# The last image's depthwise convolution with its tiles in turn, its layernorm in two parts, weight factors on ScalarE and one product block moved later

## The chip, the core and the metric

The kernel runs on one core of a Trainium2 chip. Its time is device time in microseconds (us) for one execution. Before the change it is 3458.06 us, the median of three runs (3454.50 to 3460.47). All numbers of a profile come from one more execution, which the profiler recorded.

Engines are called by their short names: PE (TensorE, matrix products), DVE (VectorE), ACT (ScalarE), POOL (GpSimd) and SP (SyncE, which issues almost all DMAs). Each engine takes its own instructions in program order.

## What is computed

Two layers follow each other on 8 images of 384 channels and 32 x 32 pixels, all in float32. Layer 0 is a transformer block over the 1024 pixels of an image. Layer 1 is a ConvNeXt block with a 7 x 7 depthwise convolution and a global response normalization (GRN). Cut to what matters here:

```python
# layer 0, for each image: tokens n = 1024, channels c = 384, 8 heads of 48
x1 = x + proj(softmax(q @ k.T * scale) @ v)        # q, k, v from layernorm(x)
x  = x1 + gelu(layernorm(x1) @ w_fc1 + b_fc1) @ w_fc2 + b_fc2   # hidden 1536
# layer 1, for each image
y = depthwise_conv7x7(x, dw_w) + dw_b              # 49 taps for each channel
y = layernorm(y) * ln_w + ln_b                     # over channels
y = gelu(y @ w1 + b1)                              # hidden 1536
gx = sqrt(sum(y * y, over pixels)); nx = gx / (mean(gx) + eps)
y = gamma * (y * nx) + beta + y
out = x + y @ w2 + b2
```

The GRN makes the last product wait for the whole image: `nx` needs the sum of squares over all pixels. The kernel does not multiply `y` by `1 + gamma * nx`, but the rows of w2, which is the same.

## The kernel before

Channels lie on partitions: an image is three tiles (`CT` = 3) of 128 channels by 1024 pixels. PE multiplies 128 x 128 weights with at most 512 pixels at a time; one such float32 product is counted as `U` = 0.857 us in the code and appears as two MATMUL records in the trace. Layer 1 of an image (here called block b) is worked on while layer 0 of the next image runs, so that DVE's convolution lies beside PE's attention. For the last image (block 7) nothing follows beside which its convolution could lie. That end of the program, from 3000 us on, is what the change is about.

**What sets the order.** Every engine's order is fixed when the program is built, by the class `Flow`. It counts PE time (`flow.pe(us)` after each matmul). Other work is written as generators ("chains") that yield how many us of PE time are to pass before their next step; a chain's next instructions are emitted when PE's count has come that far. `flow.finish(chain)` emits what is left of a chain at once. So a yield time that is too short for the engine makes it fall behind PE, and one that is too long leaves it idle. A chain started by `after(first, chain)` begins when `first` is through.

**The convolution** (L777 to L789) is 49 taps for each of three tiles. Each tap is one DVE instruction on the zero-padded image `pad`: dst = window * tap + dst (L788; the first, L786, adds the bias). For blocks 0 to 6 it runs over whole tiles of 1024 pixels in the order tap by tap, and in each tap over the three tiles (`acc` in the trace). Block 6's taps are spaced 1.5 us of PE time apart (`start_conv`), the first 10 taps of each tile 1.35 times as much.

For block 7 the destination is `last` (a view of the tile `wqkv`, whose weights are no longer needed). The last image's layer 0 MLP runs by halves of the pixels (`mlp_by_halves`, L746): first fc1 and fc2 for pixels 0 to 511, then for 512 to 1023. After each of its three output tiles, DVE evicts PE's bank into `x` (L708), ACT copies the half tile into `pad` (L704), and `between(h, ct)`, which is `last_convolution` (L1217), starts a chain with all 49 taps of that tile for the rows that have become possible: rows 0 to 12 in the first half (416 pixels), rows 13 to 31 in the second (608). Each chain waits for the one before, so the 49 taps of one tile follow one another, each on the result of the one before. After the last fc1 product of the first half, `between(0, -1)` calls `next_norms(7)`, which finishes block 6's convolution and starts its layernorm.

**The layernorm** (L331): two DVE adds over the three tiles (L344, L345), a matmul with ones for the sum over partitions (ln_sum, L348), three DVE subtractions (L352), three ACT squares (L357), two DVE adds (L361, L362), a matmul (ln_var, L365), ACT's Ln and Exp (L373, L374, which need a table load of ACT), three DVE products (L377). `abreast` runs two of them step by step together, the second in borrowed space. The last image's pixels are cut in three parts, `LAST`, of 416, 288 and 320 pixels. The first part has its own layernorm (norm_a), the other two go abreast when the convolution is over (norm_b).

**The end of the program on PE:** block 6's up-projection (h, L296; `grn_up_straight`), block 7's up-projection of the first 416 pixels (h_last, L936; `last_up`), block 6's down-projection (o, L892; `grn_down_straight`: three row blocks r by two halves, each 12 products, with the rows in pairs of weight tiles A11 A12, A21 A22, A31 A32), block 7's up-projection of the 288 and 320 pixels alternating (36 products of each), then block 7's down-projection in nine blocks. After each up-projection matmul group ACT does a Gelu (L328) and a square with a running sum (L869, L942), which gives GRN's sums. `grn_scale` (L945) then takes the square root on ACT, sums over partitions on PE (gxsum, L951), makes the factor on DVE (gmean to gscale, L954 to L959), and `scaled` (L966) multiplies each w2 tile by it on DVE (L969, 128 x 768).

**Memory that gates the order:** weights pass through a ring of 9 tiles; `weights.used` frees one and SP issues the load of the next in the plan. PSUM has four banks for half tiles (`o_tile`) and two double banks (`linear`), handed out in turn, so a matmul group waits until the group four (or two) before it has been read. The residual rows pass through three `res` tiles.

The lines that call these at the end:

```python
                norm_b = flow.spawn(after(state["conv"], last_norm(*LAST[1:])))
                y, gx = grn_up_straight(b - 1, acc, weights, b - 1)
                scale = flow.spawn(grn_scale(b - 1, gx, weights, b - 1, RAW[:2]))
                flow.finish(state["norm_a"])
                ...
                last_up(last, y_last, LAST[:1], sums, weights, f"{b}_0")
                flow.finish(scale)
                ...
                grn_down_straight(b - 1, halves, kept.pop(b - 1), weights, b - 1, b - 1)
        flow.finish(state["conv"])
        flow.finish(norm_b)
        last_up(last, y_last, LAST[1:], sums, weights, f"{B - 1}_1")
        ...
        flow.finish(grn_scale(B - 1, gx, weights, B - 1, RAW[:2]))
        grn_down_straight(B - 1, y_last, kept.pop(B - 1), weights, B - 1, B - 1, LAST)
```

Of the kernel before, what the change touches and what calls it, by code (L numbers as in the profile page):

```python
# [47 lines left out]
ALU = mybir.AluOpType  # L48
# [82 lines left out]
def block_kernel(  # L131
# [75 lines left out]
    def image(ap):  # L207
        return ap.rearrange("p (h w) -> p h w", h=H)
# [537 lines left out]
    def mlp_by_halves(b, xt, xn, weights, ln, rest, between):  # L746

        hid = one.tile([P, HT * N], F32, tag="big", name=f"hid_{b}").rearrange("p (m n) -> p m n", m=HT)
        for h in range(2):
            wa, wb = f"fc1_{b}_{h}", f"fc2_{b}_{h}"  # L750
            flow.finish(ln)
            for m in range(HT):
                gelu_half(hid, m, h, xn, weights, wa, f"fc1_{b}")
                if m % CM == CM - 1:
                    weights.used(wa, m // CM)
                if m == 3 and h == 0:
                    rest()
                    ln = flow.spawn(layernorm(xt, xn, 1, eps0, "g2", f"ln2_{b}", True))
            if h == 0:
                between(0, -1)  # L760
            for ct in range(CT):
                keys = RAW[2 * ct : 2 * ct + 2]
                tiles = [weights.at(wb, key)[:, k, :] for key in keys for k in range(6)]
                ps = linear_half(lambda k: tiles[k], lambda k: hid[:, k, :], HT, h, f"fc2_{b}_{ct}_{h}")
                for key in keys:
                    weights.used(wb, key)
                add_first(xt, ct, h, ps)
                pad_half(xt, ct, h)
                between(h, ct)
# [4 lines left out]
        nc.sync.dma_start(out=kept.rearrange("(c p) n -> p c n", p=P), in_=xt)  # L774
        return kept

    def convolution(acc, us, slow=0, y0=0, y1=H, tiles=range(CT)):  # L777

        for i in range(KS * KS):
            dy, dx = divmod(i, KS)  # L780
            for ct in tiles:
                window = pad[:, ct, dy + y0 : dy + y1, dx : dx + W]
                dst = image(acc[:, ct, :])[:, y0:y1, :]
                tap = col("dww", ct * KS * KS + i)
                if i == 0:
                    nc.vector.tensor_scalar(dst, window, tap, col("dwb", ct), ALU.mult, ALU.add)  # L786
                else:
                    nc.vector.scalar_tensor_tensor(dst, window, tap, dst, ALU.mult, ALU.add)  # L788
                yield us * (1.35 if i < slow else 1.0)  # L789

    def block_differences(acc):

# [77 lines left out]
            weights.used(f"w1_{tag}", i, "A")  # L870
        return y, gx

    def grn_down_straight(b, y, kept, weights, tag, index, parts=(slice(0, NH), slice(NH, N))):

        todo = [(r, part) for r in range(CT) for part in parts]
        res = {}

        def load():
            if len(res) < len(todo):
                r, part = todo[len(res)]  # L880
                t = three.tile([P, NH], F32, tag="res", name=f"res_{b}_{r}_{part.start}")[:, : part.stop - part.start]
                nc.sync.dma_start(out=t, in_=kept[r * P : (r + 1) * P, part])
                res[len(res)] = t

        for _ in range(3):
            load()
        for n, (r, part) in enumerate(todo):
            keys = RAW[2 * r : 2 * r + 2]
            tiles = [weights.at(f"w2_{tag}", key)[:, k, :] for key in keys for k in range(HT // 2)]
            ps = o_tile(f"o2_{b}_{r}")[:, : part.stop - part.start]  # L890
            for k in range(HT):
                nc.tensor.matmul(out=ps, lhsT=tiles[k], rhs=y(k, part), start=(k == 0), stop=(k == HT - 1))  # L892
                flow.pe(U * (part.stop - part.start) / NH)
                if k == 2 and part is parts[0] and r + 1 < CT:
                    for key in RAW[2 * r + 2 : 2 * r + 4]:
                        scaled(b, weights.at(f"w2_{tag}", key), key)
            if part is parts[-1]:
                for key in keys:
                    weights.used(f"w2_{tag}", key)
            nc.vector.scalar_tensor_tensor(res[n], ps, b2[:, r : r + 1], res[n], ALU.add, ALU.add)  # L900
            nc.sync.dma_start(out=image_of(out, index)[r * P : (r + 1) * P, part], in_=res[n])
            load()
# [22 lines left out]

        return at

    def last_up(acc, y, parts, gx, weights, tag):

        for i in range(HT // 2):  # L930
            raw = weights.at(f"w1_{tag}", i, "A")
            for m, tiles in ((i, (0, 1, 2)), (i + HT // 2, (5, 3, 4))):
                for part in parts:
                    ps = o_tile(f"h_last_{m}_{part.start}")[:, : part.stop - part.start]
                    for k in range(CT):
                        nc.tensor.matmul(  # L936
                            out=ps, lhsT=raw[:, tiles[k], :], rhs=acc[:, k, part], start=(k == 0), stop=(k == CT - 1)
                        )
                        flow.pe(U * (part.stop - part.start) / NH)
                    other_table(y(m, part), ps, AF.Gelu, bias=b1[:, m : m + 1])  # L940
                    sums = gx[:, LAST.index(part), m : m + 1]
                    nc.scalar.activation(ps, y(m, part), AF.Square, accum_out=sums)  # L942
            weights.used(f"w1_{tag}", i, "A")

    def grn_scale(b, gx, weights, tag, first=("A31", "A32")):  # L945

        wb = f"w2_{tag}"
        other_table(gx, gx, AF.Sqrt)
# [10 lines left out]
        nc.vector.tensor_scalar(scale, scale, 1.0, None, ALU.add)  # L959
        row_scale[b] = scale  # L960
        for key in first:
            scaled(b, weights.at(wb, key), key)

    row_scale = {}

    def scaled(b, w, key):  # L966
        s = (int(key[2]) - 1) * HT // 2
        factors = row_scale[b][:, s : s + HT // 2].unsqueeze(2).to_broadcast((P, HT // 2, P))
        nc.vector.tensor_tensor(w, w, factors, ALU.mult)  # L969
        return w  # L970
# [169 lines left out]
    def main():  # L1140
# [18 lines left out]
        for b in range(1, B):  # L1159
# [6 lines left out]
            if b == B - 1:  # L1166
                plan += plan_w1(f"{b}_0", False)
            plan += plan_w2(b - 1, b < B - 1)
        weights = Weights(plan + plan_w1(f"{B - 1}_1", False) + plan_w2(B - 1, False))

        t = three.tile([P, 2, NH], F32, tag="p", name="wqk_beta1").rearrange("p a n -> p (a n)")[:, : 2 * C]
        for k in range(CT):
# [12 lines left out]
            state["acc"] = one.tile([P, CT, N], F32, tag="acc", name=f"acc_{b}")  # L1185
            state["conv"] = flow.spawn(convolution(state["acc"], us, slow), paced=True)

        def next_norms(b):

            if b > 0:  # L1190
                acc = state["acc"]
                flow.finish(state["conv"])
                norm = abreast(acc, acc, eps1, "lnw", f"ln3_{b - 1}", True)
                state["norm3"] = flow.spawn(sequence(norm, block_differences(acc)) if b < B - 1 else norm)
            if b + 1 < B:
                xn = state["xn"] = load_x(b + 1, "xn")
                state["norm1"] = flow.spawn(
# [10 lines left out]

        last = wqkv[:, : CT * N].rearrange("p (c n) -> p c n", c=CT)

        def last_norm(*parts):
            args = last, last, eps1, "lnw", f"ln3_{B - 1}", True
            if len(parts) == 2:
                return abreast(*args, parts=parts)
            return layernorm(*args[:2], *parts, *args[2:], slow=2.0)

        def last_convolution(h, ct):  # L1217
            if ct < 0:
                next_norms(B - 1)
                return  # L1220
            rows = (LAST[0].stop // W, H) if h else (0, LAST[0].stop // W)
            state["conv"] = flow.spawn(
                after(state["conv"], convolution(last, 0.86 if h else 0.6, 0, *rows, (ct,))), paced=True
            )
            if (h, ct) == (0, CT - 1):
                state["norm_a"] = flow.spawn(after(state["conv"], last_norm(LAST[0])))

        for b in range(B):
            qT, kT, last_tile = qk(b, state["xn"])
# [19 lines left out]
            flow.finish(state["norm3"])  # L1249
            if b < B - 1:  # L1250
                y, y1, gx = grn_up(b - 1, acc, weights, b - 1)
                start_conv(b, 1.5 if b == B - 2 else 1.8, 10)
                scale = flow.spawn(grn_scale(b - 1, gx, weights, b - 1))
                next_values(b + 1)
                flow.finish(scale)
                grn_down(b - 1, y, y1, kept.pop(b - 1), weights, b - 1, b - 1)
            else:

                norm_b = flow.spawn(after(state["conv"], last_norm(*LAST[1:])))
                y, gx = grn_up_straight(b - 1, acc, weights, b - 1)  # L1260
                scale = flow.spawn(grn_scale(b - 1, gx, weights, b - 1, RAW[:2]))
                flow.finish(state["norm_a"])
                sums = small.tile([P, CT, HT], F32, tag="gx_last", bufs=1, name="gx_last")
                y_last = places()
                last_up(last, y_last, LAST[:1], sums, weights, f"{b}_0")
                flow.finish(scale)
                halves = lambda k, part: y[:, k, part]
                grn_down_straight(b - 1, halves, kept.pop(b - 1), weights, b - 1, b - 1)
        flow.finish(state["conv"])
        flow.finish(norm_b)  # L1270
        last_up(last, y_last, LAST[1:], sums, weights, f"{B - 1}_1")
        gx = sums[:, 0, :]
        for i in range(1, CT):
            nc.vector.tensor_tensor(gx, gx, sums[:, i, :], ALU.add)
        flow.finish(grn_scale(B - 1, gx, weights, B - 1, RAW[:2]))
        grn_down_straight(B - 1, y_last, kept.pop(B - 1), weights, B - 1, B - 1, LAST)

    engines = {nc.tensor.engine, nc.vector.engine, nc.scalar.engine, nc.gpsimd.engine, nc.sync.engine}
    with tc.manual_schedule(engines=engines):
# [129 lines left out]
```

## Time and profile before

| what | value |
|---|---|
| median of the runs | 3458.06 us |
| profiled execution: its time, its span | 3456.23 us, 3454.4 us |
| mean granted PE clock | 0.994 of full speed |
| PE busy in the span | 3390.3 us (98%) |
| DVE busy | 2510.1 us (73%) |
| ACT busy | 1293.2 us (37%) |
| DVE busy from 3171.7 to 3322.5 us | 145.3 of 150.8 us |
| PE busy in the same stretch | 132.3 us, clock 0.94 |
| first matmul of block 7's down-projection, end of its last | 3382.58 us, 3446.46 us |

The span is the time from the first to the last instruction of the profiled execution; its time is 1.8 us more. A line of a timeline gives the start in us from the span's start, the duration of the group, engine and line of the code, the operation, and what is written and read (tile names, partitions x elements), with the number of instructions; in square brackets stands how long the engine was idle before, and whose end released it. In a list of waits the columns are who waited, for whom, the sum in us, how often, and the longest. A row by stretches has the stretch, its length, the busy time of an engine with the number of instructions, and the granted PE clock, 1.00 being full speed.

### The profile page before, as it was taken

What the parts mean: (1) busy time and instruction counts of PE and PEld (TensorE: products, weight loads), DVE (VectorE), ACT (ScalarE), POOL (GpSimd) and SP (SyncE); (2) the same over time, 40 slices, a digit from 0 to 9 for tenths busy, and PEclk for the clock granted to TensorE, in tenths of its full rate; (3) what the DMA queues carried; (4) which work ended last, traced back from release to release, by engine and by line L of the source; (5) the groups of instructions that cost most, each with busy time, mean ns of one, the idle gap of its engine ahead of it and who ended that gap; (6) DMA issues with size and microseconds to landing.
All of it is one profiled execution on the core that took longest, in us unless ns stands there. A gap on an engine that the chain in (4) does not pass through costs nothing.

```text
span 3454.4 us, 36387 instructions
## 1 busy us (share of the span) xinstructions
PE 3390.3 (98%) x14278; PEld 1454.9 (42%) x14278; DVE 2510.1 (73%) x3100; ACT 1293.2 (37%) x1669; POOL 23.0 (1%) x45
## 2 busy tenths in 40 slices
PE   8999999999999999999999999999999999999988
PEld 3444434443344433444334443444434443344445
DVE  3334797787867868679686787857887789979951
ACT  3442453414434154251542415333253324532421
POOL 0100000000000000000000000000000000000000
PEclk9999999999999999999999999999999999999999
DMA  3313101321013210232002220131201221022120
GB/s 116 118 40 88 44 17 54 101 75 26 17 58 111 66 20 13 69 101 69 18 17 75 90 73 13 31 107 58 60 17 54 93 72 37 17 66 75 55 75 32
DMA packets 105283, 201.68 MB, mean 58 GB/s; under 512 B 30864, under 2 KB 33296, under 8 KB 104720
## 3 DMA queue, kind: packets, MB, share of 16 engines
q1 hardware_dynamic: 102224, 185.79, 18.5%
q0 software_dynamic: 2304, 11.01, 1.0%
q8 instruction: 114, 1.87, 0.2%
q10 hardware_dynamic: 576, 2.48, 0.2%
q14 instruction: 65, 0.53, 0.1%
HBM read 160.95 MB, written 28.57 MB: 55 GB/s over the span
## 4 chain that ended last, share of the span: by engine, by line
PE 83%; DVE 13%; DMA 2%; issue 1%; SPq 1%; ACT 1%; DVEq 0%; ACTq 0%
PE fc L309 11%; PE s L512 11%; PE o L532 11%; PE h L316 10%; DVE wqkv L788 6%; PE qk L296 6%; PE fc_straight L652 4%; PE fc_S L316 4%; PE v L441 4%; PE o_S L316 4%; PE o_straight L652 4%; DVE acc L788 3%; PE fc_A L316 3%; PE o_A L316 3%; PE proj L455 3%; PE o L892 2%
## 5 line engine op out<-in xcount | busy, mean ns | idle before, releaser
L788 DVE SCALAR_TENSOR_TENSOR acc<-pad,vec,acc 128x1024 f32<-128x1024 f32 x1008 | 1234.9, 1275 | 0.0
L521 ACT ACTIVATE p<-s 128x1024 f32<-128x1024 f32 x512 | 523.1, 1023 | 383.0 <-PE s L512 382.6
L512 PE MATMUL s<-qk 48*64 48x512 f32 x4096 | 536.4, 593 | 2.5 <-ACT qk L415 1.5
L532 PE MATMUL o<-p,v 64*64 64x512 f32 x4096 | 531.1, 590 | 0.0
L309 PE MATMUL fc<-xn,fc 128*128 128x512 f32 x1152 | 502.5, 594 | 2.7 <-DVE x L708 2.7
L309 PEld LDWEIGHTS fc<-xn,fc 128*128 128x128 f32 x1152 | 218.7, 190 | 281.5 <-issue 272.2
L512 PEld LDWEIGHTS s<-qk 48*64 48x64 f32 x4096 | 151.7, 133 | 296.5 <-issue 270.1
L532 PEld LDWEIGHTS o<-p,v 64*64 64x64 f32 x4096 | 156.4, 133 | 284.4 <-issue 279.4
L835 DVE TENSOR_TENSOR y<-h,y 128x512 f32<-128x512 f32 x288 | 197.7, 690 | 95.7 <-PE h L316 89.6
L328 ACT ACTIVATE hid<-fc,bfc_f 128x512 f32<-128x512 f32 x192 | 130.9, 686 | 360.4 <-PE fc L309 360.3
L788 DVE SCALAR_TENSOR_TENSOR wqkv<-pad,vec,wqkv 128x416 f32<-128x416 f32 (+1 forms) x288 | 216.5, 752 | 9.7
L296 PE MATMUL qk<-xn,wqkv 128*128 128x512 f32 x480 | 207.4, 592 | 0.0
L316 PE MATMUL h<-acc,w_A 128*128 128x512 f32 x432 | 205.9, 592 | 0.0
L415 ACT ACTIVATE qk<-qk,bqk 128x1024 f32<-128x1024 f32 x40 | 44.5, 1114 | 352.6 <-DVE acc L788 177.3
L473 DVE TENSOR_TENSOR attn<-o,attn 128x512 f32<-128x512 f32 x64 | 44.1, 689 | 147.5 <-ACT attn L471 147.2
L652 PE MATMUL fc_straight<-hid,fc_A 128*128 128x512 f32 x336 | 147.5, 592 | 0.0
L296 PEld LDWEIGHTS qk<-xn,wqkv 128*128 128x128 f32 x480 | 91.1, 190 | 114.1 <-issue 113.8
L441 PE MATMUL v<-wqkv,xn 128*128 128x384 f32 x384 | 128.5, 493 | 0.6 <-DVE xn L377 0.6
L455 PE MATMUL proj<-attn,wproj_sb 128*128 128x512 f32 x288 | 127.6, 596 | 0.6 <-DVE attn L499 0.6
L704 ACT COPY pad<-x 128x512 f32<-128x512 f32 x48 | 30.4, 634 | 257.3 <-DVE x L733 152.7
L316 PEld LDWEIGHTS h<-acc,w_A 128*128 128x128 f32 x432 | 82.1, 190 | 103.3 <-issue 86.1
L652 PE MATMUL o_straight<-y,w_A 128*128 128x512 f32 x288 | 124.6, 592 | 0.0
(232 smaller groups left out, 3419.7 us busy)
## 6 DMA issues: line engine op xcount, KB each, us to landing
w_A<-in_w SPq DMA_DIRECT2D x102, 384.0 KB, 3.3
fc<-in_wfc SPq DMA_DIRECT2D x54, 384.0 KB, 3.3
fc_A<-in_wfc SPq DMA_DIRECT2D x47, 384.0 KB, 3.3
xn<-in_x SPq DMA_DIRECT2D x16, 768.0 KB, 6.9
x<-in_x SPq DMA_DIRECT2D x16, 768.0 KB, 6.4
kept<-x SPq DMA_DIRECT2D x8, 1536.0 KB, 5.8
fc_S<-s_fc SPq DMA_DIRECT2D x28, 384.0 KB, 3.2
res<-kept SPq DMA_DIRECT2D x42, 256.0 KB, 3.2
```

What stands on the lines that cost most here:

```text
L296: nc.tensor.matmul(out=ps[:, half(h)], lhsT=lhsT(k), rhs=rhs(k)[:, half(h)], start=(k == 0), stop=(k == nk - 1),)
L309: nc.tensor.matmul(out=ps, lhsT=lhsT(k), rhs=rhs(k)[:, half(h)], start=(k == 0), stop=(k == nk - 1))
L316: nc.tensor.matmul(out=bank, lhsT=lhsT, rhs=rhs, start=k == 0, stop=k == len(pairs) - 1)
L328: nc.scalar.activation(dst, src, function, **kw)
L441: nc.tensor.matmul(out=ps[:, :C], lhsT=xn[:, k, t * P : (t + 1) * P], rhs=wv_sb[:, k, :], start=(k == 0), stop=(k == CT - 1),)
L455: nc.tensor.matmul(out=ps, lhsT=wproj_sb[:, m, ct * P : (ct + 1) * P], rhs=attn[:, m, :], start=(m == 0), stop=(m == CT - 1),)
L512: nc.tensor.matmul(out=s[64 * i : 64 * i + 64, j, :], lhsT=kT[64 * j : 64 * j + HD, m, k0 : k0 + 64], rhs=qT[64 * j : 64 * j + HD, m, half ...
L521: nc.scalar.activation(p, s, AF.Exp)
L532: nc.tensor.matmul(out=outs[i][64 * j : 64 * j + 64, :], lhsT=v[keys, t, at : at + 64], rhs=p[keys, j, :], start=(t == 0), stop=(t == KT - 1),
L652: nc.tensor.matmul(out=straight[:, n, :], lhsT=a(key)[k], rhs=block(s, n)[k], start=s + k == 0, stop=s == 1 and k == h - 1,)
L788: nc.vector.scalar_tensor_tensor(dst, window, tap, dst, ALU.mult, ALU.add)
L835: nc.vector.tensor_tensor(dst, bank, part, ALU.add)
```

## The change

1. The convolution gets a list `ready` of tiles that grows while it runs. At each step it takes, among the ready tiles that still have taps left, the one with the fewest taps done, but not the tile of the step before if another has taps left. For blocks 0 to 6 all three are ready at once. For block 7 there is one chain for each half, started with its first tile; the others join when their pad copy has been emitted.
2. Block 6's taps are spaced 1.42 us instead of 1.5.
3. `between(0, -1, ln)`, with block 6's layernorm, is called after m == 6 of the first half's fc1 instead of after m == 11, and that layernorm follows the one of the last image's second half.
4. Norm_b takes the 288 pixels alone, and a new norm_c the 320 pixels after it. Accordingly `last_up` does the 288 pixels first and then, with weights loaded a second time, the 320.
5. Factors of w2 in these last two blocks, except those of the tile A11, are multiplied on ACT, in six instructions of 128 x 128 for each tile.
6. The last of block 6's six down-projection blocks (r = 2, pixels 512 to 1023) is done after the last up-projection, with its two weight tiles loaded and multiplied a second time; block 7's `grn_scale` is spread beside it.

Cut to its core:

```diff
-            if h == 0:
-                between(0, -1)
+                if m == 6 and h == 0:
+                    between(0, -1, ln)
...
-        for i in range(KS * KS):
+        done = [0] * CT
+        ct, n = None, 0
+        while min(done) < KS * KS:
+            left = [c for c in ready if done[c] < KS * KS]
+            ct = min([c for c in left if c != ct] or left, key=lambda c: done[c])
+            i = done[ct]
             dy, dx = divmod(i, KS)
-            for ct in tiles:
...
-                if k == 2 and part is parts[0] and r + 1 < CT:
+                if k == 2 and rows.index(r) == n and r + 1 in rows:
                     for key in RAW[2 * r + 2 : 2 * r + 4]:
-                        scaled(b, weights.at(f"w2_{tag}", key), key)
+                        scaled(b, weights.at(f"w2_{tag}", key), key, True)
...
-    def scaled(b, w, key):
+    def scaled(b, w, key, spare=False):
         s = (int(key[2]) - 1) * HT // 2
+        if spare:
+            for k in range(HT // 2):
+                nc.scalar.mul(w[:, k, :], w[:, k, :], row_scale[b][:, s + k : s + k + 1])
+            return w
...
+        plan += plan_w1(f"{B - 1}_1", False) + plan_w1(f"{B - 1}_2", False)
+        plan += plan_w2(f"{B - 2}_b", False)[4:] + plan_w2(B - 1, False)
...
+                norm = sequence(norm, block_differences(acc)) if b < B - 1 else after(ln, norm)
...
+            ready[h].append(ct)
+            if ct == 0:
+                rows = (LAST[0].stop // W, H) if h else (0, LAST[0].stop // W)
+                conv = convolution(last, 0.86 if h else 0.6, 0, *rows, ready[h])
+                state["conv"] = flow.spawn(after(state["conv"], conv), paced=True)
...
-                start_conv(b, 1.5 if b == B - 2 else 1.8, 10)
+                start_conv(b, 1.42 if b == B - 2 else 1.8, 10)
...
-                norm_b = flow.spawn(after(state["conv"], last_norm(*LAST[1:])))
+                norm_b = flow.spawn(after(state["conv"], last_norm(LAST[1], 1.0)))
+                norm_c = flow.spawn(after(norm_b, last_norm(LAST[2], 1.2)))
                 y, gx = grn_up_straight(b - 1, acc, weights, b - 1)
-                scale = flow.spawn(grn_scale(b - 1, gx, weights, b - 1, RAW[:2]))
+                scale = flow.spawn(grn_scale(b - 1, gx, weights, b - 1, RAW[:2], RAW[1:2]))
...
+                blocks = [(r, half(n)) for r in range(CT) for n in range(2)]
+                args = b - 1, halves, kept[b - 1], weights
+                grn_down_straight(*args, b - 1, b - 1, blocks[:-1])
         flow.finish(state["conv"])
         flow.finish(norm_b)
-        last_up(last, y_last, LAST[1:], sums, weights, f"{B - 1}_1")
+        last_up(last, y_last, 1, sums, weights)
+        flow.finish(norm_c)
+        for key in RAW[4:]:
+            scaled(B - 2, weights.at(f"w2_{B - 2}_b", key), key, True)
+        last_up(last, y_last, 2, sums, weights)
...
+        scale = flow.spawn(grn_scale(B - 1, gx, weights, B - 1, RAW[:2], RAW[1:2]))
+        grn_down_straight(*args, f"{B - 2}_b", B - 2, blocks[-1:])
+        flow.finish(scale)
+        blocks = [(r, part) for r in range(CT) for part in LAST]
+        grn_down_straight(B - 1, y_last, kept[B - 1], weights, B - 1, B - 1, blocks)
```

The matmuls are the same in number and shape. The order of every engine's instructions up to the start of block 6's convolution is the same.

## The prediction

> **What bounds the kernel now.** I read the page's busy shares first (PE 98% of the span), then PE's waits, then the timelines of PE, VectorE (DVE) and ScalarE (ACT) from 3000 us on, last the granted clock around each wait. PE's order is fixed by the program, so the end moves only by what PE idles and by the clock it gets. PE's waits from 3000 us on:
>
> ```profile
> PE ln_sum L348 <- DVE ln_a L345: 13.6, 1, 13.6
> PE h L296 <- ACT h L869: 6.7, 1, 6.7
> PE gxsum L951 <- ACT gx_last L328: 2.7, 1, 2.7
> PE fc L309 <- DVE x L708: 2.7, 1, 2.7
> PE o L892 <- DVE w_A L969: 2.2, 1, 2.2
> PE ln_var L365 <- DVE ln_sq L362: 1.8, 1, 1.8
> PE h_last L936 <- DVE wqkv L377: 1.3, 1, 1.3
> ```
>
> The columns after the colon are total, times and longest. They sum to 31.0 us, and four cool the clock after them (TensorE timeline by stretches: us, busy, clock, DMA, GB/s):
>
> ```profile
> 3102.31:3104.00 1.69, 1.69 (x3) 0.58 0.00 0
> 3104.00:3106.00 2.00, 2.00 (x4) 0.50 0.00 0
> 3177.00:3179.00 2.00, 2.00 (x4) 0.50 0.95 301
> 3198.20:3200.00 1.80, 1.80 (x5) 1.00 0.00 0
> 3325.00:3327.00 2.00, 2.00 (x4) 0.50 0.04 8
> 3382.50:3384.50 2.00, 1.92 (x3) 0.50 0.00 0
> ```
>
> Multiplying each stretch by what its clock lacks gives 1.7 after the wait of 2.7, 2.85 after 6.7, 2.4 after 13.6, 1.7 after 2.7 + 2.2; the 1.84 before 3198.2 cooled nothing. So 31.0 + 8.65 = 39.7 us is all that this end could give. DVE stands behind four of the waits, at ln_sum, ln_var and fc directly, at h by way of ACT, whose Gelu is queued behind a pad copy that waits for DVE's L708. From 3071 to 3323 DVE is busy with taps of the last convolution (DVE timeline: start, us, group):
>
> ```profile
> 2870.07 37.15 DVE L788 SCALAR_TENSOR_TENSOR acc<-pad,vec,acc 128x1024 f32<-128x1024 f32 x31
> ...
> 3110.34 32.96 DVE L788 SCALAR_TENSOR_TENSOR wqkv<-pad,vec,wqkv 128x416 f32<-128x416 f32 x48
> ...
> 3212.99 1.78 DVE L377 SCALAR_TENSOR_TENSOR wqkv<-wqkv,vec,ln_rstd 128x416 f32<-128x416 f32 x3
> ...
> 3227.92 22.15 DVE L788 SCALAR_TENSOR_TENSOR wqkv<-pad,vec,wqkv 128x608 f32<-128x608 f32 x25
> 3249.99 0.16 DVE L954 TENSOR_REDUCE gmean<-gxsum 128x1 f32<-128x12 f32 x1
> ```
>
> **A tap in turn: rule and row.** A tap lasts 0.652 us (416 wide), 0.852 (608), 1.277 (1024). On one tile the next starts later than the end: (32.96-0.65)/47 = 0.687 and (22.15-0.85)/24 = 0.887. Block 6's taps, which go round three tiles, come every (37.15-1.28)/30 = 1.196, 81 ns before the end; the three L377, the same operation on 416 elements of three tiles, every (1.78-0.65)/2 = 0.566. Against this change speaks the Trainium skill, "VectorE: DVE Perf Modes", section "The DRAIN you can't avoid": the next operation starts only when the pipe is empty, leaving out semaphores between chained operations gains nothing[...]. By that rule taps in turn stay at 0.687/0.887, and the change gives nothing here. The L377 row is the same instruction without a dependence, so I take it: 0.566, and 0.852-0.083 = 0.769 for 608 wide. Saved: 0.12 us on each of some 128 + 147 taps = 33 us of DVE. The first 18 taps have one tile ready and keep 0.687.
>
> **Part by part.** Positions are from the instruction order of the changed program, durations from the rows; times are on the old axis, without the first item's shift.
>
> Block 6's taps at 1.42 instead of 1.5: the taps lie beside attention, whose last steps on DVE and PE are these:
>
> ```profile
> 3018.49 0.68 DVE L473 TENSOR_TENSOR attn<-o,attn 128x512 f32<-128x512 f32 x1
> ...
> 3028.22 0.69 DVE L499 TENSOR_TENSOR attn<-attn,r 128x512 f32<-128x512 f32 x1 [1.82 <-DMA r<-back]
> ```
>
> ```profile
> 3027.30 7.95 PE L455 MATMUL proj<-attn,wproj_sb 128*128 128x512 f32 x18
> ```
>
> DVE gets three taps earlier into the down stage (its 3.48 us of idle before L473 at 2910.7 takes them), then one more (1.2) before L361 at 2986.6. There ln_var already waits 0.47 us for L362, so PE loses 1.2. Between there and the L473 shown stand two more taps than before (2.4), and the reciprocals, each a tap later, let two L499 wait for their `r` (1.2): L473 starts 3.6 later. The taps that stood between it and the L499 shown are gone, but what they hid, the round from L473 through DMA, reciprocal and DMA, stays at 9.7 us. L499 ends near 3032.5. PE's proj needs it from its third product on: 3027.3 + 1.2 + 2 x 0.86 = 3030.2. So PE waits 2.3 more. Bounds: 0 (SP gets the round done sooner) and 5. I take **+3.5**.
>
> Norms spawned after m == 6: PE's ln_sum pair stands 5.1 us earlier, at 3056.5; DVE has its sums at 3054.6, no wait. For the last image this step loads nothing, so no queue of DMAs moves. The pair of ln_var (1.7) now precedes the first eviction L708, and the first tap comes at 3072.7 instead of 3071.1.
>
> First part in turn: 18 taps and six L377 put the second L708 at 3089.1. The next tap reads that tile's pad copy and stands directly behind: it waits for ACT's 0.63, as does the third tile's (0.75 each). 17 taps at 0.566: third L708 at 3100.25, PE goes on at 3101.05 instead of 3102.31. That wait falls from 2.7 to 1.45, shorter than the 1.84 that cooled nothing: **-1.25-1.7**. Then 68, 17 and 18 taps put the second half's L708 at 3140.3, 3150.6 and 3161.5 (before: 3147.3, 3159.5, 3171.7). ACT's pad copy, Gelu and square (0.63+1.1+1.2) free PE's bank at 3165.2; PE asks at 3165.6. **-6.7-2.85**, by a margin of 0.4. The statistics of the first part take 11 and 7 taps on DVE: L362 ends 3185.3, PE asks 3183.5, so that wait stays: **0**.
>
> w2's factors on ACT: DVE loses five products of 0.87 (4.4 us). Of the ACT form there is no row: per instruction between 0.21 (128x12) and 0.41 (128x288), on the line through 288 and 1024 columns 0.27, with a pointer operand some 0.06 more, less overlap; I take 0.29, six for a block: 1.75 (1.3 to 2.5). In the new order A12's six stand on ACT behind h_last_1 and wait for DVE's gscale. DVE reaches it after 17 + 41 taps, at 3232.6; ACT is free 4 us earlier. Queued behind: the Gelu of h_last_7, whose bank PE asks for at 3233.2 and gets at 3232.6+1.75+1.2 = 3235.6: **+2.4** (0 to 6, by DVE's lag). A21 to A32 run on ACT beside 41 us of PE's products.
>
> The end of the convolution: from here PE leads. DVE waits at each L900 eviction, then needs 12 taps (9.2) against PE's 10.3. L345 ends at 3294.2; PE asks at 3297.9. **-13.6-2.4**.
>
> Norm in two parts: PE has nothing beside the first. From its sixth product's end come eviction, two adds, ln_var, Ln and Exp, first L377: 0.8+1.0+0.5+1.1+0.6 = 4.0, of which PE works 0.5. Idle 3.5 in place of 1.3, **+2.2**. Clock: the skill's "TensorE: Matmul & The Clock Gate", section "What's actually happening", puts the cooling after an idle window of about 3.4 us; these are two halves of 1.75, so by the rule nothing cools. The nearest row is 2.74 + 2.18 idle with 0.4 of work between, which ended at 0.50, and a single 2.7 did too. I take the row: **+1.7**. For the waits of 2.3 and 2.4 above, between 1.84 (kept) and 2.7 (cooled), I take 0; they are 1.7 each for the range. The second part's norm lies within the 17.6 us of 36 products 288 wide. ACT there has 12x1.07 of Gelu and square, three squares, two table loads, Ln and Exp: 17.7, nearly PE's time, and then twelve factors (3.5); one bank comes late: **+0.7**.
>
> One block later: 12 products of 0.857 = 10.3 us of PE now cover Sqrt, gxsum, gscale and the first factor (5.3 us between 3377.3 and 3382.6). **-4.9-1.7**. What is late next is A11's product, ready 1.2 us early. PE's products are otherwise the same. SP issues eight more weight loads (384 KB, 3.3 us to landing); the ring frees each 4.7 us or more ahead of its use: 0. The last `res` load stands behind six of them and still has 10 us.
>
> Sum: 3.5-2.95-9.55+2.4-16.0+3.9+0.7-6.6 = **-24.6**. The profiled execution took 3456.2 us (span 3454.4 and 1.8 around it): 3431.6. The median shown is 1.8 higher; I predict **3433 us**.
>
> **Rivals.** (a) The rule holds, taps in turn gain nothing: DVE still paces. It saves 4.4 (factors) and loses 1.5 (pad copies), 1.7 (first tap) and 3.5 (attention): L344 starts at 3324.4 instead of 3322.05, and ACT's wait for gscale disappears under that. From there: sums 0.9, ln_sum and two products at half clock 3.4, norm 4.0, the two up-projections 40.6 (17.6 + 19.5 + 1.1 of sums + 0.7 + 1.7), the kept block and gxsum 10.6, the last products 62.2 (63.9 less the cooling): 3446.1 against 3446.5: **3456**, no change. For it: the rule; against it: both rows. (b) Slower: a tap in turn, which waits for a semaphore of its own tile two back, comes later than a tap on one tile. Place: L788 from 3071 to 3323; price: 2.9 us for each 10 ns; slower by 0.2% from 24 ns above today's pitch, at 30 ns **3465**. Nothing but the rule speaks for it; 31 taps in turn show the opposite. (c) The new waits are dearer: 2.3 and 2.4 both cool (+3.4), ACT's factors take 2.5 (+2), the margin of 0.4 at h is missed (+2): **3441**. For it: margins under a microsecond. (d) They are not there: no wait at proj (-2.3), no cooling at the norm (-1.7), gscale 2 us sooner (-2): **3427**.
>
> **How the numbers follow.** Forecast 0.62 (its own range 3427 to 3439), (c) 0.15, (d) 0.16, (a) 0.04, (b) 0.03. The range 3423 to 3444 takes in (c) and (d) with 3 us around. 0.2% is 6.9 us, about what a measurement of this kernel tells from no change: faster 0.93, same 0.04, slower 0.03.
>
> **What would show it.** Runs of 128x416 and 128x608 taps at 0.57 and 0.77 a piece; no PE wait of 13 us at ln_sum nor of 6 at h; gxsum without a wait; new PE waits at proj on L499, in the first up-projection on ACT behind the factors, and before the 288-wide one. Wrong if taps keep 0.69/0.89, or if ACT waits over 6 us for gscale.

## The result, and the profile after

The changed kernel takes 3433.72 us (median of 4 runs, 3431.39 to 3434.99), beside 3457.44 us for the kernel before on the same chip: a ratio of 0.9931, 95% interval 0.9913 to 0.9948. The time predicted was 3433 us. The profiled execution took 3434.99 us (span 3433.2, mean PE clock 0.996, PE busy 3387.9 us). That a sum comes out right does not say that its terms were, so the terms are taken one by one below; three of them were not.

First PE's waits of the changed kernel, from 3000 us on as before:

```profile
PE ln_var L365 <- DVE ln_sq L362: 2.7, 2, 1.8
PE proj L455 <- DVE attn L499: 2.4, 1, 2.4
PE h_last L945 <- DVE wqkv L377: 1.6, 1, 1.6
PE fc L309 <- DVE x L708: 1.2, 1, 1.2
PE h_last L945 <- ACT h_last L950: 0.6, 1, 0.6
```

The 13.6 us at ln_sum, the 6.7 at h and both waits at the last GRN (2.7 and 2.2) are gone. New are proj, and the two halves of the wait around the norm of the 288 pixels (1.8 at ln_var, 1.6 at h_last). The sum falls from 31.0 to 8.5 us. (L788, L892 and L936 of before are L794, L901 and L945 now.)

The taps, in DVE's timeline, and then the 288 taps of the last convolution as one group of the page, before and after (busy us, mean ns of one, idle us before):

```profile
3111.51 37.77 DVE L794 SCALAR_TENSOR_TENSOR wqkv<-pad,vec,wqkv 128x416 f32<-128x416 f32 x67
...
3208.28 31.34 DVE L794 SCALAR_TENSOR_TENSOR wqkv<-pad,vec,wqkv 128x608 f32<-128x608 f32 x41
```

```profile
L788 DVE SCALAR_TENSOR_TENSOR wqkv<-pad,vec,wqkv 128x416 f32<-128x416 f32 (+1 forms) x288 | 216.5, 752 | 9.7
L794 DVE SCALAR_TENSOR_TENSOR wqkv<-pad,vec,wqkv 128x416 f32<-128x416 f32 (+1 forms) x288 | 193.4, 745 | 0.6
```

A tap lasts almost as long as before (745 ns in the mean against 752), but the next one starts sooner: (37.77 - 0.65) / 66 = 0.562 us apart for 416 pixels, (31.34 - 0.85) / 40 = 0.762 for 608, where 0.687 and 0.887 stood. A group's mean of one would have hidden this; its busy time shows it (216.5 us before, 193.4 now), and so does the length of a run of taps.

To see where the time went, cut the program at four places that both programs have: the first qk product of image 7, the first fc product after the last proj, the first h_last product, and the first product of block 6's down-projection. The table gives what each stretch has more or less than in the profile of before, in us, for the prediction and for three profiles of the changed kernel (b1 and d1 are runs of it made with the experiments):

| stretch (length before) | predicted | after | b1 | d1 |
|---|---|---|---|---|
| start to image 7's qk (2862.4) | 0 | +4.3 | +0.8 | +4.0 |
| attention and proj (172.7) | +3.5 | +5.1 | +3.0 | +4.0 |
| MLP by halves, block 6's up-projection (198.2) | -12.5 | -13.8 | -13.8 | -13.8 |
| h_last 416 wide, with gscale (25.4) | +2.4 | +0.3 | +0.3 | +0.3 |
| from block 6's down-projection on (187.9) | -18.0 | -16.8 | -16.5 | -18.0 |
| sum from qk on | -24.6 | -25.2 | -27.1 | -27.5 |

The first row is no part of the change: over the 14 profiles of this study, of ten programs, image 7's qk starts between 2860.8 and 2869.3 us, and the profile of before had one of the early starts. That is why the spans of the two profiles differ by 21.2 us only. Most of this spread goes with the clock: in the first 180 us the mean granted clock is 0.98 in the three profiles with the least half-clock time there (before, b1, d2), whose qk starts at 2860.8 to 2863.2 us, and 0.95 in the four with the most (a3, b3, b4, d1), whose qk starts at 2866.4 to 2869.3 us.

### The profile page after: what moved, and what is told of

Read it like the earlier page. It is cut to its first block, busy times and chain, and to the rows that moved or that the text cites. A ratio compares the mean times of both kernels' runs of the same rounds, so it can differ in the third digit from the quotient of the medians.

```text
span 3433.2 us, 36479 instructions
## 1 busy us (share of the span) xinstructions
PE 3387.9 (99%) x14278; PEld 1454.8 (42%) x14278; DVE 2479.7 (72%) x3090; ACT 1315.5 (38%) x1743; POOL 23.0 (1%) x45
## 4 chain that ended last, share of the span: by engine, by line
PE 86%; DVE 10%; DMA 2%; ACT 1%; SPq 1%; issue 1%; DVEq 0%; ACTq 0%
PE fc L309 11%; PE s L512 11%; PE o L532 10%; PE h L316 10%; PE qk L296 6%; PE fc_S L316 4%; PE fc_straight L652 4%; DVE acc L794 4%; PE v L441 4%; PE o L901 4%; PE o_S L316 4%; PE o_straight L652 4%; PE fc_A L316 3%; DVE wqkv L794 3%; PE o_A L316 3%; PE proj L455 3%
## 5 line engine op out<-in xcount | busy, mean ns | idle before, releaser
L794 DVE SCALAR_TENSOR_TENSOR acc<-pad,vec,acc 128x1024 f32<-128x1024 f32 x1008 | 1234.9, 1275 | 0.0
L794 DVE SCALAR_TENSOR_TENSOR wqkv<-pad,vec,wqkv 128x416 f32<-128x416 f32 (+1 forms) x288 | 193.4, 745 | 0.6
```

## Experiments

Each kernel is the changed one with an edit, unless something else is said. Times are medians; "before" ran beside them on the same chip (3457.1 us for a1 to a4, 3460.1 for b1 to b4, 3457.4 for c1, 3461.4 for d1 to d3), so kernels are compared within one letter, and across letters by the stretches of the trace.

### Taps one after another, and taps in turn alone

a1 takes the turns away (`ready` is a list for the last image alone):

```diff
-            ct = min([c for c in left if c != ct] or left, key=lambda c: done[c])
+            if isinstance(ready, list):
+                ct = left[0]
+            else:
+                ct = min([c for c in left if c != ct] or left, key=lambda c: done[c])
```

> The changed kernel, but the last image's taps follow one another on one tile as before (49 taps of one tile, then the next); all else stays. If taps in turn are what freed DVE, taps go back to 0.687 us (416 wide) and 0.887 us (608 wide), DVE paces the end again, PE waits at ln_sum by some 12 us or more and at h by some 6 us, and the time is 3455 to 3461 us. If the pitch does not depend on the order of the tiles, runs of taps stay near 0.56 and 0.76 us and the time stays at 3434 us.

Measured: 3457.23 us, ratio to before 0.9997 (0.9989 to 1.0006). Its DVE timeline and its waits:

```profile
3118.33 32.97 DVE L797 SCALAR_TENSOR_TENSOR wqkv<-pad,vec,wqkv 128x416 f32<-128x416 f32 x48
...
3235.91 23.04 DVE L797 SCALAR_TENSOR_TENSOR wqkv<-pad,vec,wqkv 128x608 f32<-128x608 f32 x26
```

```profile
PE h L296 <- ACT h L880: 10.4, 1, 10.4
PE h_last L948 <- DVE gmean L966: 4.8, 1, 4.8
...
PE ln_sum L348 <- DVE ln_a L345: 2.5, 1, 2.5
```

(32.97 - 0.65) / 47 = 0.688 us and (23.04 - 0.85) / 25 = 0.888: the old distances, in the program with all other items of the change. The time is that of the rival (a) that said taps in turn gain nothing (3456 us). The waits came in other places than I expected: 10.4 us at h rather than 6, 4.8 at gmean, where I had named none, and 2.5 at ln_sum rather than 12. Before ln_sum PE had thus been held for 15 us, and DVE was that much less behind it there.

a2 is the other half: the kernel before with item 1 only (the functions `convolution` and `last_convolution` of the change).

> The kernel before with item 1 of the change alone (taps in turn); spacing 1.5, block 6's layernorm after m == 11, the norm of the last two parts abreast, factors on DVE and all six product blocks before the last up-projection stay as before. By the steps of the prediction this alone takes away the waits at ln_sum (13.6 us and 2.4 of clock), at h (6.7 and 2.85), some 3 us at fc and 0.9 at ln_var: 29 us less than before, 3428 us, that is faster than the whole change, whose other items then cost some 5 us together. Rival: DVE is still late at ln_sum without the factors moved to ACT and the earlier norm of block 6, so that some of the wait remains: 3436 us or more.

Measured: 3431.62 us, ratio 0.9925 (0.9909 to 0.9942); the whole change has 0.9931, 0.9919 and 0.9921 on its three chips, so item 1 alone does as well. From image 7's qk to the end its trace has 27.6 us less than before. I had expected 3428 us, 29 less than before. These waits were left:

```profile
PE gxsum L959 <- ACT gx_last L328: 2.7, 1, 2.7
PE h L296 <- ACT h L877: 2.3, 1, 2.3
PE o L900 <- DVE w_A L977: 2.2, 1, 2.2
```

The wait at h shrank from 6.7 to 2.3 us but did not go. In every other run with taps in turn it is gone; of these a3 differs from a2, up to that place, only in having block 6's norm after m == 6, and its MLP stretch (184.4 us) is 1.6 us shorter. That is what item 3 brings. The other two waits are the GRN's, untouched. So item 1 carries the gain, and items 2 to 6 together neither add nor take anything that can be measured.

### The spacing of block 6's taps

a3 and d2 are the same kernel:

```diff
-                start_conv(b, 1.42 if b == B - 2 else 1.8, 10)
+                start_conv(b, 1.5 if b == B - 2 else 1.8, 10)
```

> The changed kernel with block 6's taps spaced 1.5 us again instead of 1.42. In the trace after, PE loses 1.2 us more at ln_var, waits 2.4 us at proj for L499 and then runs 3.3 us at half clock (1.7 lost). If the spacing is the cause, proj has no wait of 2 us, the clock stays at 1.00 there and the time is 5.3 us less: 3428 to 3429 us. Rival: the earlier place of block 6's layernorm needs the closer spacing (taps left over are issued in a lump before it), so PE waits at ln_sum of block 6 or at fc instead and the time is 3434 us or more.

> The changed kernel beside the next two on one chip, since medians of one kernel differed by 2 us from chip to chip. Expected: 24 to 28 us under before, with a loss in the attention (against spacing 1.5) of 2 to 7 us that changes from profile to profile.

> The changed kernel with spacing 1.5, on the same chip as d1. If item 2 costs what the traces say (2.3 to 6.8 us, 4 in the mean), it is 3 to 6 us faster than d1; if a3's lower median was its chip, it is within 1.5 us of d1.

Measured: a3 3426.27 us, 2 us under its band; d1 3432.66 (28.7 under before, a little more than expected) and, on the same chip, d2 3428.04 us, 4.6 less than d1. The stretch of attention and proj takes 172.4 to 173.0 us in all six profiles with 1.5 (a2, a3, b4, c1, d2, d3; before: 172.7), and 177.8, 175.7, 174.9, 175.7, 179.4, 176.2, 176.6 in the seven with 1.42 (after, a1, a4, b1, b2, b3, d1): 2.2 to 6.8 us more, 4.0 in the mean. (The intervals of the ratios of d1 and d2, 0.9908 to 0.9935 and 0.9895 to 0.9926, overlap; it is the stretch of the trace, without an exception in 13 profiles, that tells the two spacings apart.) PE's waits of a3 have no line of proj:

```profile
PE ln_var L365 <- DVE ln_sq L362: 2.7, 2, 1.8
PE h_last L945 <- DVE wqkv L377: 1.6, 1, 1.6
PE fc L309 <- DVE x L708: 1.2, 1, 1.2
PE h_last L945 <- ACT h_last L950: 0.6, 1, 0.6
```

The rest of the trace is the same with either spacing, so item 2 gives nothing back: it is a loss of some 4 us. The rival, that the earlier norm needs the closer spacing, falls.

### The factors

In a4 `scaled` does all tiles on DVE again (`spare = False` in its first line).

> The changed kernel with all factors of w2 on DVE again. DVE gets five more products of 0.87 to 0.96 us (4.4 to 4.8 us) before the layernorm of the 288 pixels; in the trace after it idles 1.05 us at L909 evictions in this stretch and its sums are 3.7 us ahead of PE at ln_sum. So the theory that DVE has that much room says no change beyond 1 us: 3433 to 3435 us, with a wait of 0 to 1 us at ln_sum. Rival: the move to ACT is part of the gain, then ln_sum waits by the whole 4.4 us and the clock cools: 3439 us.

Measured: 3428.97 us, under the band I gave; the ratio, 0.9917 (0.9901 to 0.9934), is within the interval of the changed kernel's, so no difference is shown. DVE's last sum before the norm, and PE's ln_sum, in a4:

```profile
3300.22 0.46 DVE L345 TENSOR_TENSOR ln_a<-ln_a,wqkv 128x288 f32<-128x288 f32 x1
```

```profile
3301.38 0.65 PE L348 MATMUL ln_sum<-ln_a,ones 128*128 128x288 f32 x2
```

DVE is through 0.7 us before PE asks; in the profile after it is 3.7 us ahead (3300.6 and 3304.31). The factors' 4.4 us on DVE took 3 us of that lead and the 1.05 us of idle time at L909, and cost PE nothing. What the move costs is the line `h_last <- ACT h_last: 0.6`, twelve factors that stand on ACT before a Gelu; a4 has no such wait. The stretch from block 6's down-projection on takes 169.1 us in a4, 171.1, 171.4 and 169.9 in the three profiles of the changed kernel; 0.65 of the difference is this wait; most of the rest is clock (see the last section).

### The block that was moved, and the norm in two parts

b2 does all six blocks before the last up-projection (item 6 undone):

```diff
-        plan += plan_w2(f"{B - 2}_b", False)[4:] + plan_w2(B - 1, False)
+        plan += plan_w2(B - 1, False)
...
-                grn_down_straight(*args, b - 1, b - 1, blocks[:-1])
+                grn_down_straight(*args, b - 1, b - 1, blocks)
...
-        for key in RAW[4:]:
-            scaled(B - 2, weights.at(f"w2_{B - 2}_b", key), key, True)
...
-        grn_down_straight(*args, f"{B - 2}_b", B - 2, blocks[-1:])
```

> The changed kernel as it is, on the same chip as the next three. In the traces so far the same wait of 1.6 to 1.8 us before the 288-wide products was followed by two, one, one and no windows of 3.41 us at half clock, and the attention, with the same instructions, took 5.1, 3.1 and 2.3 us more than before. If this is where in a grid of windows of 3.41 us the waits fall, the single runs spread over some 4 us and the median is 3431 to 3434 us, and this profile may show another number of slow windows. If the cooling were fixed by the program, proj and the norm show the same 3.4 and 6.8 us at 0.50 again.

> The changed kernel with item 6 undone: all six product blocks of block 6 stand before the last up-projection, w2's last two tiles are loaded and multiplied once. By the prediction's sum alone the waits at gxsum (2.7), at o (2.2) and 1.7 of clock come back: 6.6 us more, 3440 us. But the norm of the 288 pixels (3.4 us of idle PE and 1.7 or more of clock in the trace after) then lies beside 12 more products, and the 0.65 us wait behind ACT's factors goes: if that cover is what the block was worth where it stood, the net is 0.5 to 1.5 us: 3433 to 3436 us, with no PE wait at ln_var 288 nor before h_last 288.

Measured: b1 3431.61, b2 3430.80 us, the latter under my band of 3433 to 3436. From block 6's down-projection on, b2 takes 170.6 us, the changed kernel 169.9 to 171.4. The waits of b2 from proj on that are over 2 us:

```profile
PE proj L455 <- DVE attn L499: 3.5, 1, 3.5
PE gxsum L960 <- ACT gx_last L328: 2.7, 1, 2.7
PE o L901 <- DVE w_A L982: 2.2, 1, 2.2
```

gxsum and o are back, as the prediction priced them, but the lines of the norm (1.8 and 1.6) and of the factors (0.6) are gone: twelve more products lie beside the norm. With the norm where it is, the block covers only one of the two gaps, and moving it from one to the other is worth nothing.

b3 keeps the moved block and does the norms of the 288 and 320 pixels abreast:

```diff
-                norm_b = flow.spawn(after(state["conv"], last_norm(LAST[1], 1.0)))
-                norm_c = flow.spawn(after(norm_b, last_norm(LAST[2], 1.2)))
+                args = last, last, eps1, "lnw", f"ln3_{B - 1}", True
+                norm_b = flow.spawn(after(state["conv"], abreast(*args, parts=LAST[1:])))
+                norm_c = None
```

> The changed kernel with item 4 undone in the norm alone: the norms of the 288 and the 320 pixels go abreast as before, both through before the 288-wide products start; the order of the products stays. Six subtractions, squares, and products in place of three each, and two of each of the rest, stand between the sums and the first 288-wide product, of which only 1.7 us of block 6's products and two more sums lie beside. I expect 3.5 to 5 us more idle before the 288-wide products and one more slow window: 3437 to 3441 us. Rival: the norm in parts is worth nothing, since ACT and DVE work in parallel in both: 3432 to 3434 us.

Measured: 3433.96 us (3428.37 to 3434.78) beside b1's 3431.61 (3429.60 to 3433.80), and 171.0 us in that stretch: no difference, as the rival had it. I expected 3.5 to 5 us more idle time; PE's timeline of b3 has this:

```profile
3309.73 1.33 PE L365 MATMUL ln_var<-ln_sq,ones 128*128 128x288 f32 x2 [4.05 <-DVE ln_sq L362]
3310.85 1.31 PE L365 MATMUL ln_var<-attn,ones 128*128 128x320 f32 x2
3312.68 5.51 PE L945 MATMUL h_last<-wqkv,w_A 128*128 128x288 f32 x15 [0.51 <-DVE wqkv L377]
```

4.05 + 0.51 = 4.6 us instead of 1.77 + 1.62 = 3.4, and the 0.6 behind ACT's factors is absent. In b3's trace ACT squares the first part from 3306.86 us on while DVE subtracts in both until 3308.75: the two engines work side by side, so the second part is nearly free.

### A version that beats both

In the profile after, DVE's sums for the 288 pixels were 3.7 us ahead of PE, yet PE idled 3.4 us for the rest of that norm. So I put the blame on the place of ln_sum in PE's order, 2 products before the end of the blocks. b4 moves it to 8 products before (`late` is 0.05 here, for the last 67 taps of the second half):

```diff
-                start_conv(b, 1.42 if b == B - 2 else 1.8, 10)
+                start_conv(b, 1.5 if b == B - 2 else 1.8, 10)
...
-            yield us * (1.35 if n <= CT * slow else 1.0)
+            yield us * (1.35 if n <= CT * slow else 1.0) - (late if n > 80 else 0)
...
-                norm_b = flow.spawn(after(state["conv"], last_norm(LAST[1], 1.0)))
+                norm_b = flow.spawn(after(state["conv"], last_norm(LAST[1], 0.5)))
...
-            scaled(B - 2, weights.at(f"w2_{B - 2}_b", key), key, True)
+            scaled(B - 2, weights.at(f"w2_{B - 2}_b", key), key)
```

> A version meant to beat both: the changed kernel with block 6's taps at 1.5 us again, the two w2 tiles that are multiplied a second time done on DVE (idle there), and the last 67 taps spaced 0.81 us instead of 0.86 with shorter steps in the norm of the 288 pixels, so that its ln_sum stands 8 instead of 2 products before the end of block 6's blocks, since DVE's sums were ready 3.7 us before PE asked. If the idle time there is only a matter of where the norm stands, the two waits (3.4 us) and their clock (1.7 to 2.7) go, at most 0.6 us of new wait at ln_sum: 5 us under the kernel with 1.5 spacing (3426.3), 3421 us. Rival: DVE is not ready and PE waits at ln_sum or at gmean by 3 us or more: 3425 us or more.

Measured: 3423.78 us, ratio 0.9890 (0.9873 to 0.9906), between the 3421 us I expected and the rival's 3425. One wait was left before the 288-wide products:

```profile
3305.46 5.12 PE L945 MATMUL h_last<-wqkv,w_A 128*128 128x288 f32 x20 [1.27 <-DVE wqkv L377]
```

c1 and d3 have `late` 0.036 and the norm's steps at 0.2 instead of 0.5.

> The early norm of b4 with shorter steps between ln_sum and ln_var: in that trace DVE had L362 ready 2.6 us before PE came to ln_var 288, and the eviction L909 of the last block, which waits for PE, stood before L377 on DVE. Here ln_var stands 3 instead of 2 products before the end of the blocks and L377 before that eviction. If this order is all that was left, the wait of 1.27 us before the 288-wide products goes and the time is 1 to 1.5 us under b4's 3423.8: 3422 to 3423 us. Rival: ACT's table load and Ln, Exp are the bound after ln_var, then over 1 us of the wait stays and the time is the same as b4's.

> The version of c1 on the same chip as d1 and d2. By the trace of c1 it has 7 us less than spacing 1.5 alone (3.4 of idle time at the norm of the 288 pixels, 1.9 of clock, 0.65 at the last up-projection and rests): 6 to 8 us faster than d2 and 10 to 12 us faster than d1. Rival: half of that was c1's chip: 3 to 4 us faster than d2.

Measured: c1 3417.32 us, ratio 0.9893 (0.9876 to 0.9909); d3 3420.48 us, ratio 0.9885 (0.9870 to 0.9900), on one chip 7.6 us under d2 and 12.2 under d1. From image 7's qk on, c1 and d3 have 38.4 and 38.2 us less than before, b4 36.3. So the new order is worth some 2 us over b4; that c1's median lies 5 us under my band is for the rest its chip and start. PE's timeline of d3:

```profile
3292.16 0.65 PE L348 MATMUL ln_sum<-ln_a,ones 128*128 128x288 f32 x2
3292.65 3.60 PE L901 MATMUL o<-y,w_A 128*128 128x512 f32 x8
3296.08 0.65 PE L365 MATMUL ln_var<-ln_sq,ones 128*128 128x288 f32 x2
3296.57 2.74 PE L901 MATMUL o<-y,w_A 128*128 128x512 f32 x6
3299.14 3.07 PE L945 MATMUL h_last<-wqkv,w_A 128*128 128x288 f32 x12
```

Four products stand between ln_sum and ln_var, three more before the first 288-wide one, and no line has an idle time in brackets. Items 5 and 6 may pay here: the moved block covers the GRN (the 2.7 and 2.2 us of b2 are absent) while the earlier blocks cover the norm, and with the factors on DVE the lead in a4 was 0.7 us, too little for a ln_sum some 5 us earlier. But no run takes either item out of this version, so this is argued, not shown.

## Why the prediction was right

**Taps in turn: right, and it is the gain.** The row of three independent L377 (0.566 us apart) was the right one to take against the rule; measured 0.562 and 0.762 against 0.566 and 0.769. a1 and a2 show it from both sides. A tap that reads the result of the one before starts 35 ns after its end, one that does not some 80 ns before it. (Taps in turn differ in the tile they write as well; no run separates the two.) My reading of the rule was half of it: the Trainium skill, "VectorE: DVE Perf Modes", section "The DRAIN you can't avoid", goes on that a next operation that is not held back starts earlier, and the rows fit that sentence. Rival (a) rested on the half that I quoted.

**The waits in the MLP: right.** fc 1.2 instead of 1.45, h without a wait, ln_var at 416 pixels 0.9 where I left 1.8; -13.8 us against -12.5.

**gscale, +2.4: wrong, +0.3.** DVE came to gmean as late as I said, and ACT waited for it (first line: PE's stretch before; all others: after):

```profile
3240.43 18.40 PE L936 MATMUL h_last<-wqkv,w_A 128*128 128x416 f32 x52
...
3236.02 18.67 PE L945 MATMUL h_last<-wqkv,w_A 128*128 128x416 f32 x52
...
3239.55 0.15 DVE L963 TENSOR_REDUCE gmean<-gxsum 128x1 f32<-128x12 f32 x1
...
3240.67 1.86 ACT L979 ACTIVATE w_A<-w_A,gscale 128x128 f32<-128x128 f32 x6 [2.83 <-DVE gscale L968]
3242.44 0.59 ACT L328 ACTIVATE v<-h_last,b_f 128x416 f32<-128x416 f32 x1
```

The six factors took 1.86 us (predicted 1.75). The failed step is "the Gelu of h_last_7, whose bank PE asks for at 3233.2": PE did not ask for that bank then. PE's 52 records of this stretch took 18.67 us against 18.40 before. The one that was late starts at 3239.76 us, 0.2 us late and released by the end of gmean at 3239.70; the next two groups of products, from 3241.96 and 3244.05 on, did not wait. So the bank that PE asks for here is that of gxsum, which DVE frees, and not that of h_last_7, which ACT had not begun to read before 3242.44. In a1, where DVE is later, gxsum's bank, asked for one group later there, costs the 4.8 us at gmean. I had counted banks strictly in turn, as the section on the kernel before has it; here they are not.

**Attention, +3.5: the waits right in the mean, the clock left out.** In the seven profiles with 1.42 spacing PE lost 0.6 to 1.4 us up to ln_var (predicted 1.2), and proj waited 2.4, 1.7, 0, 1.7, 3.5, 1.9 and 2.6 us (predicted 2.3). "For the waits of 2.3 and 2.4 above, between 1.84 (kept) and 2.7 (cooled), I take 0" failed at the first of these. The same fourteen records of proj, after and in d1:

```profile
3036.84 7.83 PE L455 MATMUL proj<-attn,wproj_sb 128*128 128x512 f32 x14 [2.41 <-DVE attn L499]
```

```profile
3036.92 6.28 PE L455 MATMUL proj<-attn,wproj_sb 128*128 128x512 f32 x14 [2.56 <-DVE attn L499]
```

After, they ran partly at half clock and took 1.55 us more. Over the seven the stretch is 4.0 us longer in the mean.

**Norm in two parts, +2.2 + 1.7: the first right, the second too small.** Its lines in PE's timeline after:

```profile
3304.31 0.65 PE L348 MATMUL ln_sum<-ln_a,ones 128*128 128x288 f32 x2
3304.80 1.88 PE L901 MATMUL o<-y,w_A 128*128 128x512 f32 x4
3308.45 0.75 PE L365 MATMUL ln_var<-ln_sq,ones 128*128 128x288 f32 x2 [1.77 <-DVE ln_sq L362]
3310.82 7.41 PE L945 MATMUL h_last<-wqkv,w_A 128*128 128x288 f32 x18 [1.62 <-DVE wqkv L377]
```

1.77 + 1.62 = 3.4 us idle (predicted 3.5). The eighteen records take 7.41 us where 0.244 each, the pace of the later ones, would make 4.4. By the windows in the last section the clock cost (2.25 + 3.41) x 0.5 = 2.8 us there instead of 1.7. The bank that I expected late for the twelve factors (+0.7) cost 0.6.

**One block later, -6.6: right where it stands, but no gain of the change.** gxsum and o wait no more, and A11 is ready in time. But I set the +2.2 + 1.7 and +0.7 of the norm against another part; b2 shows that they are the price of this one.

The misses (gscale 2.1 too dear, the MLP 1.3 too dear, attention and clock some 2.8 too cheap) nearly cancelled: that the sum came out within 1 us is luck. It is luck of the chip too. On the chips of b and d the same two kernels differ by 28.5 and 28.7 us, where they differ by 23.7 here and I had forecast 25; from qk on the three profiles have 25.2 to 27.5 us less.

## What to carry to other kernels

Where an engine is paced by a chain of operations on one accumulator, and others are ready, let them alternate; look for the gain in the start-to-start distance, not in the mean duration. Work moved to cover one gap uncovers another: price both places in one sum, and then move the small instruction (here ln_sum) to the cover rather than the cover to it. Undo each part of a bundle alone: here one of six items carried the gain, and a small retiming cost 4 us.

## What the clock does after a wait

I had not expected the same wait of the same program to cost nothing (d1) or 1.55 us of clock (after) at proj, and 1.6 (d1) to 3.1 us (b1) at the norm. In all 14 profiles the steps of the granted clock lie whole multiples of 3.413 us apart, on a grid that lies differently in each run. Cutting the traces along that grid shows what decides. First the norm of the 288 pixels after, then in a4 (PE alone; the clock is the number behind the count of instructions, then come DMA share and GB/s):

```profile
3306.24:3309.65 3.41, 1.19 (x4) 1.00 0.57 142
3309.65:3313.07 3.42, 2.25 (x5) 0.50 0.13 50
3313.07:3316.48 3.41, 3.41 (x9) 0.50 0.00 0
```

```profile
3305.04:3308.46 3.42, 1.33 (x4) 1.00 0.51 171
3308.46:3311.87 3.41, 3.41 (x9) 0.50 0.00 0
3311.87:3315.28 3.41, 3.41 (x15) 1.00 0.43 113
```

A window in which PE is little busy (1.19 and 1.33 of 3.41 us) is followed by one at half clock; a slow window that is not nearly full (2.25) is followed by another. After, 1.2 us of the second half of the wait fell into the slow window, so a second followed; in a4 both halves ended before the edge, and one was enough. And proj in d1, whose wait of 2.56 us is longer than the 2.41 that cooled in the profile after:

```profile
3032.67:3036.08 3.41, 1.69 (x4) 1.00 0.65 219
3036.08:3039.50 3.42, 2.58 (x6) 1.00 0.01 4
```

It lay across an edge, and nothing cooled. Over the windows from 2900 us on in all profiles: with PE's matrix products busy up to 0.39 of a full-speed window, the next was always slow; from 0.43 to 0.52 it was slow in 2 of 13; above, never. A slow window busy 0.82 or less was followed by another slow one, at 0.93 or more by a fast one. The Trainium skill, "TensorE: Matmul & The Clock Gate", section "What's actually happening", says that the window is free-running and 3413 ns long, which these traces show; it speaks of an idle window, where here a window busy for a third was enough. For a sum over waits in this kernel this means: idle time under about 1.5 us in a window (PE busy for over 0.55 of it) never cooled, over 2.1 us (busy up to 0.39) it always did, and between the two the share of busy time alone does not decide. A slow window that is full costs 1.7 us, a second one comes on top if more idle time falls into the first, and a pair of waits in one window counts as one.
